# When layer 1's table of finished rows is read, and when it is stored: eight bunches instead of six

## The chip, the cores and the metric

The kernel runs on one core of one Trainium2 chip. The core has five instruction streams that run beside each other and meet only at semaphores: PE (TensorE, matrix products, with its weight loads shown apart as PEld), DVE (VectorE), ACT (ScalarE), POOL (GpSimd, which here does nothing but issue gathers) and SP (SyncE, which here does nothing but issue plain DMAs). The metric is the device time of one execution in microseconds, the median of several runs. A profile is one further execution, recorded by the hardware; its times are microseconds from the first instruction unless marked ns.

## What is computed

A graph with 12,500 nodes of 128 features and 200,000 edges, sorted by the node they end in (`dst`), goes through two relational graph layers, a residual sum and a layer norm. An edge's type is the largest of ten of its 42 attributes.

```python
seg  = dst * NUM_REL + edge_type
sums = segment_sum(x[src], seg);  cnt = segment_sum(1, seg)
mean = (sums / maximum(cnt, 1)).reshape(N, NUM_REL, -1)
layer(x) = einsum('nrd,rdo->no', mean, w_rel) + x @ root + bias
h   = relu(layer_1(x))
out = layernorm(x + layer_2(h))
```

All of it is float32. The feature of an edge's source is fetched by its index (`x[src]`), so a gather from DRAM stands ahead of every sum.

## The kernel before

**Tiles and bunches.** The edges are cut into 1,563 tiles of 128, in the order of `dst`; four tiles (`QB`) make a bunch. For a tile, POOL gathers 128 rows, one for each edge's source (L751). DVE makes a matrix of ones and zeros from the edges' types and nodes, ACT weighs it with one over the count, PE multiplies the gathered rows with it (L983), and DVE adds the product into a ring of sums, `cc` (L797). Gathered rows stand in seven buffers (`GB`) of a bunch each, so POOL can be at most seven bunches ahead of the products.

**Blocks.** The nodes are finished in 52 blocks, most of 256 nodes, that is, about eight bunches of edges each. When the last edges of block k are surely summed, `finish(k)` runs, in the bunch that the code calls `finished_in(k)`: PE multiplies the ring's sums with the ten weight matrices (L739, L742), ACT adds the bias and cuts at zero (`shifted`, L672), PE turns the result back into rows (`rows_out`, L864), and ACT copies the rows to SBUF (`rows_kept`, L871), from where SP stores them in `hD`. Further steps follow by due times that are counted in bunches: the products of layer 2's own part (`second`, three bunches on), their store in `T2` (`second_kept`, four bunches on, L889; the trace calls it T), the clearing of the ring, the next block's features (`fetch`, one bunch on).

**The joint tables.** Layer 2 needs, for the same edges, rows of h in place of rows of x. Part of that is done along with layer 1: from tile `T0` on, POOL gathers from a table `XH` whose rows hold x and, beside it, h as far as it is finished and zeros elsewhere. One gather then feeds two products. An edge whose source is not yet finished contributes nothing to the second product; it is listed and done in layer 2 (the "second" tiles there). So that the list can be made, the kernel fixes for each block from 3 (`K0`) to 43 (`K1`) the tile from which the table is read with this block in it, `first_seen[k]`: `finished_in(k) + READY` bunches, rounded up to a row of eleven tiles (`RT`). The stretch between two such tiles is an epoch. Tiles ahead of `T0` are gathered from x alone, and are done again as a whole in layer 2 (the "plain" tiles there).

**Two copies.** There are two tables, and epochs alternate between them (`table_of`), since the table being read must not change. So each block is stored twice: into the table of its own epoch by `rows_kept` (here called the first copy), and into the other one later, by `todo_late`, two bunches after `first_seen[k]` (the second copy of block k, which the epoch of block k+1 needs). The framework lets a gather wait for all stores in its table that stand ahead of it in the program, and a store for all earlier gathers from its table. Tables are first filled with x and zeros by ACT's queue (`table_rows`, up to bunch 38).

**What sets the order.** The order of instructions on each engine is that of the code: bunch by bunch, and within a bunch POOL's gathers, PE's products, jobs (preparing the edges' types and counts for chunks of 32 bunches), DVE's sums of two bunches before, `finish`, then `todo` and `todo_late`. SP, too, works its queue strictly in this order: whatever stands ahead of a store and waits holds the store up.

**Layer 2** runs over the plain tiles, while DVE compacts the list of left-over edges, and then over the second tiles, with gathers from `hD`.

Of the kernel before, what the change touches and what calls it, by code (L numbers as in the profile page):

```python
# [30 lines left out]
QB = 4  # L31
# [19 lines left out]
SPLIT = 63  # L51
LEAD = 40
LAST = 40
READY = 6
LOW = 1 << 13
TOPN = (1 << 14) - 1
OFF = 80
# [7 lines left out]
def rgcn_resnorm_kernel(ctx: ExitStack, tc: tile.TileContext, x, src, dst, attr, w_rel1, root1, b1,  # L65
# [23 lines left out]
    NBLK = len(starts)  # L89
# [19 lines left out]
    def finished_in(k):  # L109

        return -(-done_after(k) // QB) - 1 + BEHIND

    K0, K1 = KSEEN
    NR = (NT - QB * (finished_in(K0) + READY)) // RT
    T0 = NT - RT * NR
# [4 lines left out]
    for k in range(K0, K1 + 1):  # L120
        r = max(0, -(-(QB * (finished_in(k) + READY) - T0) // RT))
        assert r < NR and (not epochs or epochs[-1][1] < r)
        epochs.append((k, r))
    rows_of = [(k, r, (epochs + [(0, NR)])[i + 1][1]) for i, (k, r) in enumerate(epochs)]
    first_seen = {k: T0 + RT * r for k, r in epochs}
# [62 lines left out]
    def bounds(t):  # L188

        return max(0, t * STEP - OFF, floor_of(t)), min(N - 1, t * STEP + OFF)  # L190
# [43 lines left out]
    def chunk_rows(c):  # L234
        return min(CT, NT - c * CT)
# [96 lines left out]
    first = float(chunk_rows(NCH - 1) * P) - 0.5  # L332
# [288 lines left out]
    def block(k):  # L621
        n0, n = ranges[-1][k]
        return n0, n, [(t, min(P, n - t * P)) for t in range(-(-n // P))]

    def rows_dma(sb, dr, k, store):
        n0, n, _ = block(k)
        full = n // P
        pairs = []
        if full:
            pairs.append((sb[:, :full], dr[n0:n0 + full * P, :].rearrange("(t p) c -> p t c", p=P)))  # L630
        if n % P:
            pairs.append((sb[:n % P, full], dr[n0 + full * P:n0 + n, :]))
        for a, b in pairs:
            nc.sync.dma_start(b, a) if store else nc.sync.dma_start(a, b)
# [3 lines left out]
    def rows_in(k):  # L638

        last = "e" if k == len(ranges[-1]) - 1 else ""  # L640
        xb = fin.tile([P, len(block(k)[2]) if last else 3, C], F32, name="xb" + last)
        rows_dma(xb, x, k, False)
        return xb

    def features_in(k, l, xb):

        n0, n, subs = block(k)
        last = "e" if k == len(ranges[-1]) - 1 else ""
        fT = fin.tile([P, (len(subs) if last else 3) * P], F32, name="fT" + last)
        if l:  # L650
            nc.sync.dma_start(fT[:, :n], hT[:, n0:n0 + n])
            return fT
        pt = ps_f.tile([P, YB], F32, name="pf")
        for t, h in subs:
            nc.tensor.transpose(pt[:, t * P:t * P + h], xb[:h, t, :], ident[:h, :h])
        nc.scalar.activation(fT[:, :n], pt[:, :n], AF.Copy)
        return fT
# [9 lines left out]
    def shifted(po, k, l):  # L667

        n = block(k)[1]
        tail = {NBLK - 1: "e", NBLK - 2: "d"}.get(k, "")  # L670
        a = fin.tile([P, P if tail else 3 * P], F32, name="a" + tail)
        nc.scalar.activation(a[:, :n], po[:, :n], AF.Identity if l else AF.Relu, bias=bsb[l])  # L672
        return a
# [15 lines left out]
    def spans(k):  # L689
        n = block(k)[1]  # L690
        return [(p, slice(a, b)) for p, a, b in ((P, 0, n // P), (n % P, n // P, -(-n // P))) if p and b > a]
# [32 lines left out]
    def folded(ls, k, w):  # L724

        if block(k)[0] % RN or not k:
            return
        s, e = cc[:, ls, :, :w], cc[:, ls, :, RN:RN + w]
        nc.vector.tensor_tensor(s, s, e, op=ALU.add)
        nc.vector.memset(e, 0.0)  # L730

    def projected(k, l, last, po=None, more=True, ring=None):

        n0, n, _ = block(k)
        o = n0 % RN
        if po is None:
            po = ps_f.tile([P, YB], F32, name="pf")
        for r in range(NREL if more else 0):
            nc.tensor.matmul(po[:, :n], wsb[l][:, r, :], cc[:, l if ring is None else ring, r, o:o + n],  # L739
                             start=(r == 0), stop=False)  # L740
        w, f = last
        nc.tensor.matmul(po[:, :n], w, f[:, :n], start=not more, stop=True)  # L742
        return po

    def stored(hb, b, k):

        rows_dma(hb, XH[b][:, C:], k, True)
# [89 lines left out]
    def layer_1():  # L837

        todo = Later()
# [4 lines left out]
        def finish(k, t):  # L844

            if k < NBLK - 2:
                todo.run(END)
            if k not in fTs:
                xbs[k] = rows_in(k)
                fTs[k] = features_in(k, 0, xbs[k])  # L850
            u = QB if t < NT else 0
            folded(ALL, k, WN)
            po = [projected(k, 0, (rsb[0], fTs[k]))]
            both = starts[k + 1] > bounds(T0)[0] if k + 1 < NBLK else True
            reused = starts[k] + RN < N
            assert not reused or t + 7 * u <= (starts[k] + RN - OFF - WN) // STEP

            def rows_out(_):
                a = po.pop()
                a = fin_a.setdefault(k, shifted(a, k, 0))  # L860
                pr = ps_f.tile([P, 4, C], F32, name="pf")
                n0, n, subs = block(k)
                for i, h in subs:
                    nc.tensor.transpose(pr[:h, i, :], a[:, i * P:i * P + h], ident)  # L864
                po.append(pr)

            def rows_kept(now):
                pr = po.pop()
                hb = fin.tile([P, 2, C], F32, name=f"hb{k % 2}")
                for p, s in spans(k):  # L870
                    nc.scalar.activation(hb[:p, s], pr[:p, s], AF.Copy)  # L871
                rows_dma(hb, hD, k, True)
                if k <= K1:
                    first = 0 if k <= K0 else (k - K0) % 2
                    stored(hb, first, k)
                    if k < K1:
                        assert k <= K0 or now + QB >= first_seen[k - 1]
                        when = t + 8 * QB if k < K0 else first_seen[k] + 2 * QB
                        todo_late.append((when, lambda t: stored(hb, 1 - first, k)))

            def second(_):
                po.append(projected(k, 1, (rsb[1], fin_a.pop(k)), more=both))

            def second_kept(_):
                n0, n, _ = block(k)
                p2 = po.pop()
                t2 = fin.tile([P, 3 * P], F32, name="v")
                nc.scalar.activation(t2[:, :n], p2[:, :n], AF.Identity, bias=bsb[1])
                nc.sync.dma_start(T2[:, n0:n0 + n], t2[:, :n])  # L889

            todo.at(t + u, rows_out)
            todo.at(t + (1 if k == NBLK - 2 else 2) * u, rows_kept)
            if reused:
                todo.at(t + 2 * u, lambda t: cleared(0, k, 0))
                todo.at(t + 3 * u, lambda t: cleared(0, k, 1))
            if k < NBLK - 1:
                todo.at(t + (9 if k >= NBLK - 3 else 3) * u, second)
                todo.at(t + (9 if k >= NBLK - 3 else 4) * u, second_kept)
            else:
                todo.run(t)  # L900
                todo.run(END)
                todo.at(t, second)
                todo.at(t, second_kept)
            if both:
                w = 10 if k >= NBLK - 3 else 5
                todo.at(t + w * u, lambda t: cleared(1, k, 0))
                todo.at(t + (w + 1) * u, lambda t: cleared(1, k, 1))
            if k + 1 < NBLK - 1:
                def fetch(t):
                    xbs[k + 1] = rows_in(k + 1)  # L910

                def turn(t):
                    n0, n, subs = block(k + 1)
                    pt = ps_f.tile([P, YB], F32, name="pf")
                    for i, h in subs:
                        nc.tensor.transpose(pt[:, i * P:i * P + h], xbs[k + 1][:h, i, :], ident[:h, :h])
                    po.append(pt)

                def turned_kept(t):
                    n0, n, subs = block(k + 1)  # L920
                    pt = po.pop()
                    fTs[k + 1] = fin.tile([P, 3 * P], F32, name="fT")
                    nc.scalar.activation(fTs[k + 1][:, :n], pt[:, :n], AF.Copy)  # L923
                todo.at(t + u, fetch)
                w = 2 if k == NBLK - 3 else 4
                todo.at(t + w * u, turn)
                todo.at(t + (w + 1) * u, turned_kept)

        fin_a = {}
        todo_late = []  # L930
# [17 lines left out]
        for p in range(-AHEAD, NPT + BEHIND):  # L948
# [9 lines left out]
            t = p * QB  # L958
# [750 lines left out]
```

## Time and profile before

| what | value |
|---|---|
| median of 3 runs | 3995.48 us (3989.87 to 4023.41) |
| the profiled execution: its own time | 4014.34 us |
| its span, first to last instruction | 4012.5 us |
| busy: PE, PEld, DVE, ACT, POOL | 2486.8, 2056.9, 2033.2, 1303.6, 2294.7 us |
| gathers from x (layer 1, to T0), first to last start | 166, 4.0 to 254.3 us |
| gathers from XH (layer 1, from T0 on) | 1397, 292.8 to 2556.9 us |
| gathers from hD, plain tiles of layer 2 | 166, 2583.0 to 2819.7 us |
| gathers from hD, second tiles of layer 2 | 695, 2844.3 to 3927.2 us |
| granted TensorE clock, mean | 0.759 |

No engine is busy for more than 62% of the span, so the time is made of waits as much as of work. In the timeline of the profile each row has the start, the duration, the engine, the line, the operation with what it writes and reads (out<-in), how many instructions were merged, and in brackets how long the engine had been idle before it and what ended that. SPq and ACTq mark instructions that issue a DMA; their duration is that of the issue, not of the transfer. "issue" and "remote" stand for waits whose end the profile does not tell. A gather's row on POOL is the making of its descriptors, and the next gather cannot start before it ends. A wait for several things is put down to the one that came last by the profile. The rows of the windows view have, for each engine, the busy time in a stretch and the number of instructions, then the granted clock, the share of time that the DMA engines worked, and GB/s.

### The profile page before, as it was taken

What the parts mean: (1) busy time and instruction counts of PE and PEld (TensorE: products, weight loads), DVE (VectorE), ACT (ScalarE), POOL (GpSimd) and SP (SyncE); (2) the same over time, 40 slices, a digit from 0 to 9 for tenths busy, and PEclk for the clock granted to TensorE, in tenths of its full rate; (3) what the DMA queues carried; (4) which work ended last, traced back from release to release, by engine and by line L of the source; (5) the groups of instructions that cost most, each with busy time, mean ns of one, the idle gap of its engine ahead of it and who ended that gap; (6) DMA issues with size and microseconds to landing.
All of it is one profiled execution on the core that took longest, in us unless ns stands there. A gap on an engine that the chain in (4) does not pass through costs nothing.

```text
span 4012.5 us, 42414 instructions
## 1 busy us (share of the span) xinstructions
PE 2486.8 (62%) x11883; PEld 2056.9 (51%) x11883; DVE 2033.2 (51%) x5464; ACT 1303.6 (32%) x3179; POOL 2294.7 (57%) x2436
## 2 busy tenths in 40 slices
PE   1555676666665666666676767624546766766666
PEld 0444565555555565555565656614444444545455
DVE  4453454555444546453444344339465555655565
ACT  2341233222332233233332323313324344444443
POOL 6645555565555565655565666466455656665661
PEclk7666777877777777777777877856768887877888
DMA  4562433343333333333333333311112122222121
GB/s 133 176 201 87 125 99 118 96 127 98 121 92 115 104 112 105 112 109 110 109 114 102 98 102 95 89 45 53 42 45 58 54 58 62 59 61 60 56 62 33
DMA packets 265374, 370.96 MB, mean 92 GB/s; under 512 B 51280, under 2 KB 197365, under 8 KB 265134
## 3 DMA queue, kind: packets, MB, share of 16 engines
q0 software_dynamic: 99920, 250.57, 21.4%
q1 hardware_dynamic: 111587, 91.97, 7.4%
q10 hardware_dynamic: 53627, 25.62, 2.2%
q8 instruction: 102, 1.67, 0.2%
q14 instruction: 138, 1.13, 0.1%
HBM read 322.86 MB, written 57.89 MB: 95 GB/s over the span
## 4 chain that ended last, share of the span: by engine, by line
PE 39%; issue 24%; another core or an unknown queue 14%; DVE 14%; ACT 2%; POOL 2%; DVEq 1%; DMA 1%; SPq 0%; ACTq 0%; POOLq 0%
PE zp L983 18%; PE pf L739 13%; DVE cc L797 5%; PE zp L1502 2%; POOL g L751 2%; DVE oh L775 2%; PE zq L1502 1%; PE pf L742 1%; ACT oh L757 1%; DVEq L782 1%; DVE oh L765 1%; DVE cc L1162 1%; PE pf L559 1%; PE pf L557 1%
## 5 line engine op out<-in xcount | busy, mean ns | idle before, releaser
L751 POOL DMA_INDIRECT g<-XH,idxE x1397 | 1321.3, 946 | 981.4 <-issue 444.6
L983 PE MATMUL zp<-oh,g 128*128 128x120 f32 x5920 | 1027.6, 327 | 727.0 <-issue 636.2
L797 DVE TENSOR_TENSOR cc<-cc,zp 128x240 f32 (+11 forms) x2193 | 841.3, 384 | 1150.6 <-remote 662.7
L983 PEld LDWEIGHTS zp<-oh,g 128*128 128x128 f32 x5920 | 943.4, 239 | 813.7 <-issue 731.8
L751 POOL DMA_INDIRECT g<-hD,idxB x695 | 657.1, 945 | 450.5 <-issue 180.6
L739 PE MATMUL pf<-cc,w 128*128 128x256 f32 (+3 forms) x3020 | 767.1, 412 | 174.9 <-issue 82.9
L739 PEld LDWEIGHTS pf<-cc,w 128*128 128x128 f32 x3020 | 616.8, 216 | 305.8 <-issue 113.5
L757 ACT ACTIVATE oh<-oh,wE 128x120 f32<-128x120 f32 x1729 | 531.2, 382 | 352.8 <-DVE oh L765 255.9
L757 ACT ACTIVATE oh<-oh,wB 128x150 f32<-128x150 f32 (+23 forms) x771 | 338.7, 482 | 442.1 <-DVE oh L775 236.4
L1502 PE MATMUL zp<-oh,g 128*128 128x120 f32 (+20 forms) x1260 | 346.8, 418 | 210.2 <-issue 79.8
L1502 PEld LDWEIGHTS zp<-oh,g 128*128 128x128 f32 x1260 | 238.4, 239 | 288.1 <-issue 212.4
L722 ACT ACTIVATE cc<-zero 128x1280 f32<-128x1280 f32 (+3 forms) x274 | 336.6, 1231 | 74.8 <-DVE cc L797 58.2
L775 DVE TENSOR_TENSOR oh<-wide,keyB 128x480 f32<-128x480 f32 (+17 forms) x400 | 230.3, 576 | 177.7 <-remote 100.3
L672 ACT ACTIVATE a<-pf,b 128x256 f32<-128x256 f32 (+1 forms) x50 | 23.2, 465 | 734.5 <-remote 313.8
L765 DVE TENSOR_TENSOR oh<-bank,keyE 128x480 f32<-128x480 f32 x391 | 253.5, 649 | 0.0
L1502 PE MATMUL zq<-oh,g 128*128 128x160 f32 (+21 forms) x614 | 183.3, 433 | 97.4 <-issue 54.9
L751 POOL DMA_INDIRECT g<-hD,idxE x166 | 157.9, 951 | 104.8 <-issue 44.5
L751 POOL DMA_INDIRECT g<-in_x_dram,idxE x166 | 156.8, 945 | 96.2 <-issue 46.9
L1502 PEld LDWEIGHTS zq<-oh,g 128*128 128x128 f32 x614 | 119.7, 229 | 147.3 <-issue 124.1
L797 DVE TENSOR_TENSOR cc<-cc,zq 128x160 f32 (+21 forms) x307 | 120.0, 391 | 61.2 <-issue 14.3
L923 ACT ACTIVATE fT<-pf 128x256 f32<-128x256 f32 (+1 forms) x50 | 18.5, 370 | 401.8 <-remote 344.6
L548 DVE TENSOR_TENSOR eqb<-bank,kh 128x1344 bf16<-128x1344 f32 (+2 forms) x65 | 100.7, 1551 | 25.4 <-remote 19.0
(241 smaller groups left out, 1288.7 us busy)
## 6 DMA issues: line engine op xcount, KB each, us to landing
m<-in_edge_attr_dram SPq DMA_DIRECT2D x48, 672.0 KB
g<-XH,idxE POOLq DMA_INDIRECT x1397
XH<-in_x_dram ACTq DMA_DIRECT2D x24, 512.0 KB
XH<-zero ACTq DMA_DIRECT2D x24, 512.0 KB
XH<-hb SPq DMA_DIRECT2D x87, 128.0 KB
g<-hD,idxB POOLq DMA_INDIRECT x695
xb<-in_x_dram SPq DMA_DIRECT2D x72, 128.0 KB
hD<-hb SPq DMA_DIRECT2D x46, 128.0 KB
```

The costliest lines, as they stand in the source:

```text
L548: nc.vector.tensor_tensor(eq[:p], kpP[:p, None, :R].to_broadcast([p, DB, R]), fore, op=ALU.is_equal)
L557: nc.tensor.matmul(pc[:p], identb[:p, :p], eq[:p, k:k + 4, L:], start=(d + k == 1), stop=False)
L559: nc.tensor.matmul(pc[:p], identb[:p, :p], back, start=False, stop=(d + k + 3 == L))
L722: nc.scalar.activation(cc[:, l, h * H:(h + 1) * H, o:o + n], zero[:, None, :n].to_broadcast([P, H, n]), AF.Copy)
L739: nc.tensor.matmul(po[:, :n], wsb[l][:, r, :], cc[:, l if ring is None else ring, r, o:o + n], start=(r == 0), stop=False)
L751: nc.gpsimd.indirect_dma_start(out=g[:, j * C:(j + n) * C], out_offset=None, in_=table, in_offset=bass.IndirectOffsetOnAxis(ap=idx, axis=0))
L757: nc.scalar.activation(s, s, AF.Copy, scale=w)
L765: nc.vector.tensor_tensor(o.rearrange("p (t m) -> p t m", m=m), cols[:, None, :m].to_broadcast([P, n, m]), keys[:, :, None].to_broadcast([ ...
L775: nc.vector.tensor_tensor(to, a, b, op=ALU.is_equal)
L797: nc.vector.tensor_tensor(s, s, z, op=ALU.add)
L983: nc.tensor.matmul(zp[:, a + l * KW:a + (l + 1) * KW], g[:, (slot[j] + l) * C:(slot[j] + l + 1) * C], oh[:, j * KW:(j + 1) * KW], start=Tr ...
L1502: nc.tensor.matmul(zp[:, j * m:(j + 1) * m], gt[:, b * C:(b + 1) * C], oh[:, j * m:(j + 1) * m], start=True, stop=True)
```

## The change

`READY` goes from 6 to 8: every `first_seen` is computed from eight bunches after the finishing in place of six. `rows_kept` is due one bunch after `finish` for every block, so it stands directly behind `rows_out`; before, it stood a bunch later except for one block. The first copy is stored there only if the table it goes into is no longer read from the next bunch on (`free`); otherwise it waits in `todo_late` until then. The assertion that made this condition a fixed one is gone. The second copy keeps its rule, two bunches after `first_seen[k]`, and moves along with that.

```diff
-READY = 6
+READY = 8
...
                 if k <= K1:
                     first = 0 if k <= K0 else (k - K0) % 2
-                    stored(hb, first, k)
+                    free = first_seen[k - 1] - QB if k > K0 else 0
+                    if now >= free:
+                        stored(hb, first, k)
+                    else:
+                        todo_late.append((free, lambda t: stored(hb, first, k)))
                     if k < K1:
-                        assert k <= K0 or now + QB >= first_seen[k - 1]
                         when = t + 8 * QB if k < K0 else first_seen[k] + 2 * QB
                         todo_late.append((when, lambda t: stored(hb, 1 - first, k)))
...
             todo.at(t + u, rows_out)
-            todo.at(t + (1 if k == NBLK - 2 else 2) * u, rows_kept)
+            todo.at(t + u, rows_kept)
```

## The prediction

> **What bounds the kernel now.** The page's groups of instructions first (busy time, mean ns, then the idle time before them), and the waits of POOL (engine, line, awaited; sum, times, longest in us):
>
> ```profile
> L751 POOL DMA_INDIRECT g<-XH,idxE x1397 | 1321.3, 946 | 981.4 <-issue 444.6
> ```
> ```profile
> POOL g L751 <- issue: 716.6, 2143, 9.7
> POOL g L751 <- remote: 284.0, 96, 10.9
> POOL g L751 <- DMA XH<-hb: 183.5, 27, 16.1
> POOL g L751 <- PE zp L983: 125.1, 38, 12.9
> ```
>
> The 1397 gathers from the joint table are 1321.3 us of work and 981.4 us of idleness. Part of the idleness is the steady step between two gathers. Another part is a wait for a block's rows: the third row says 183.5 us in 27 waits, and some of the waits put down to a product or to "issue" fall at the same places. To see the places, read POOL's timeline at the gathers that open an epoch; I show the first, a few between, and the last.
>
> ```profile
> 292.83 0.94 POOL L751 DMA_INDIRECT g<-XH,idxE  x1 [37.64 <-DMA XH<-zero]
> ...
> 348.61 0.94 POOL L751 DMA_INDIRECT g<-XH,idxE  x1 [11.10 <-DMA XH<-hb]
> ...
> 510.28 0.94 POOL L751 DMA_INDIRECT g<-XH,idxE  x1 [5.93 <-DMA XH<-hb]
> ...
> 883.75 0.94 POOL L751 DMA_INDIRECT g<-XH,idxE  x1 [3.77 <-DMA XH<-hb]
> ...
> 934.89 0.94 POOL L751 DMA_INDIRECT g<-XH,idxE  x1 [3.25 <-DMA XH<-hb]
> ...
> 974.62 0.94 POOL L751 DMA_INDIRECT g<-XH,idxE  x1 [9.75 <-PE zp L983]
> ...
> 1138.15 0.94 POOL L751 DMA_INDIRECT g<-XH,idxE  x1 [9.70 <-issue]
> ...
> 1193.07 0.94 POOL L751 DMA_INDIRECT g<-XH,idxE  x1 [9.81 <-PE zp L983]
> ...
> 2128.89 0.94 POOL L751 DMA_INDIRECT g<-XH,idxE  x1 [16.13 <-DMA XH<-hb]
> ...
> 2339.07 0.94 POOL L751 DMA_INDIRECT g<-XH,idxE  x1 [5.36 <-DMA XH<-hb]
> ...
> 2390.27 0.94 POOL L751 DMA_INDIRECT g<-XH,idxE  x1 [3.68 <-DMA XH<-hb]
> ```
>
> All 40 openings from 348.61 to 2390.27 have such a pause, 3.25 to 16.13 us, 7.2 us in the mean. One epoch shows what is waited for (block 18):
>
> ```profile
> 1077.56 0.47 ACT L672 ACTIVATE a<-pf,b 128x256 f32<-128x256 f32 x1 [12.07 <-PE zp L983]
> ...
> 1079.46 0.38 ACT L871 ACTIVATE hb<-pf 128x256 f32<-128x256 f32 x1 [0.29 <-PE pf L864]
> ...
> 1080.28 0.46 SPq L634 DMA_DIRECT2D XH<-hb  x1
> ...
> 1082.99 0.94 POOL L751 DMA_INDIRECT g<-XH,idxE  x1 [7.77 <-DMA XH<-hb]
> ...
> 1088.76 0.33 SPq L889 DMA_DIRECT2D T<-v  x1
> ```
>
> `rows_kept` at 1079.46, its store at 1080.28, and 2.25 us after the end of that issue (1082.99 − 1080.74) the gather goes on. So at each epoch POOL stands because the newest copy has not landed. But POOL's pause is not PE's. Two stretches after this very pause (the windows view: bounds, length, then PE, PEld, DVE, ACT, POOL):
>
> ```profile
> 1083.00:1092.50 9.50, 9.36 (x63) 8.57 (x62) 6.32 (x16) 3.67 (x11) 7.37 (x8) 1.00 0.70 229
> 1092.50:1105.20 12.70, 1.84 (x8) 1.21 (x7) 2.24 (x6) 0.82 (x1) 9.64 (x11) 0.68 0.35 108
> ```
>
> While POOL issues its first eight gathers, PE does 63 products in 9.5 us; in the next 12.7 us, with POOL still issuing, 8. PE and POOL take turns, and a pause of POOL's is partly paid back. What a pause costs must therefore be read from whole epochs of 33 gathers: 883.75 to 934.89 is 51.14 us, with a pause of 3.25 at its end; 1138.15 to 1193.07 is 54.92 us, with 9.81. That is 3.78 us for 6.56 us of pause, **0.576 us per us**, and 51.14 − 0.576 × 3.25 = 49.3 us for an epoch without any. 2339.07 to 2390.27 tests it: 49.3 + 0.576 × 3.68 = 51.4, measured 51.20.
>
> **The change part by part.**
>
> *How far the reading moves.* By the code's arithmetic an epoch is 33 tiles, a few 22. What decides a pause is the distance in bunches from where the later of its two copies stands in the program to the first gather that reads it. Before, both come at `finished_in` +0 to +3 and the reading at +6.0 to +8.5; the distance is 3.0 at the three openings that follow a 22-tile epoch, 4.25 to 5.25 at 16, 5.5 to 6.25 at 21. After, the first copy comes at +1 (+2 in nine, where `free` holds it back) and the reading at +8.0 to +10.5. The first copy is then 6.0 to 9.25 bunches ahead and no longer decides. The second copy does, since it moves along with `first_seen`: 5.5 to 6.25 bunches at 36 openings, 3.0 at four that follow 22 tiles. So this is not two bunches more for everybody, it is the 16 middle ones brought to where 21 others are already.
>
> *What that is worth.* The 21 openings at 5.5 to 6.25 (first 510.28, last 2390.27) pause 5.5 us in the mean; the 16 at 4.25 to 5.25 8.6 (among them 348.61, 1138.15, 1193.07); the three at 3.0, 9.75 to 16.13. After, I split the 36. In 22 of them the second copy falls at +4 or +5, in SP's queue right behind block k's T2 store (1088.76 for block 18, 8.5 us after the first copy), which waits for products as the first copy did before: I give them the same 5.5. In the other 14 nothing late stands ahead of the copy, and I give them 3.3, the longer of the pauses that POOL makes with no copy in play, seen in the last stretch of the joint gathers:
>
> ```profile
> 2412.01 0.94 POOL L751 DMA_INDIRECT g<-XH,idxE  x1 [3.29 <-remote]
> ...
> 2465.06 0.94 POOL L751 DMA_INDIRECT g<-XH,idxE  x1 [2.08 <-PE zp L983]
> ```
>
> Mean (22 × 5.5 + 14 × 3.3) / 36 = 4.6. A long epoch is then 49.3 + 0.576 × 4.6 = 51.95 us. A short one was 934.89 to 974.62 = 39.73 with 9.75 of pause; I take 40 for each of the four.
>
> *Fewer joint tiles.* `T0` goes from 166 to 177. The pause of 37.64 us at 292.83 is for the zero fill from ACT's queue, which does not move, so the joint gathers start at the same instant, with 11 of them done from x during that pause.
>
> **Sum of the stage.** Before: 2390.27 − 292.83 = 2097.44 us. After: 36 × 51.95 + 4 × 40 = 2030 us. **−67 us.** Bounds: with pauses as now (7.2 in all) the 11 tiles fewer alone are left, 36 × (49.3 + 0.576 × 7.2) + 160 = 2084, −13; with 3.0 everywhere, 36 × 51.03 + 4 × (39.73 − 0.576 × 6.75) = 1981, −117; at the pace of the last stretch (2412.01 to 2465.06, 36 gathers in 53.05 us, 1.474 each) the 1276 gathers take 1881 us, −216. I take −67 because its terms are from epochs of the same kind. The 110 joint tiles behind 2390.27 stay.
>
> *`rows_kept` a bunch sooner.* On ACT, `hb` no longer follows the next bunch's weighting. In the row at 1079.46 it had waited 0.29 us for the transposes already, so there is next to nothing to gain there; a loss is ACT standing for the transposes while weights queue behind it: from 1077.56 + 0.47 to 1079.46, 1.4 us, while PE is at the block's own products anyway. I take 0, bounds −1 to +3 us per block at 0.576. On SP, `hD` and the first copy now stand ahead of `fetch` of the next block's features; those are wanted a block later, so nothing is late.
>
> *Layer 2.* 11 tiles more are plain and 4 second tiles fewer.
>
> ```profile
> L751 POOL DMA_INDIRECT g<-hD,idxB x695 | 657.1, 945 | 450.5 <-issue 180.6
> ```
> ```profile
> 2844.30 1.01 POOL L751 DMA_INDIRECT g<-hD,idxB  x1 [23.66 <-DVE vB L1260]
> ```
>
> 11 gathers of 1.25 us (0.945 + 0.30) are 13.75 us, and lie under the 23.66 us in which POOL waits for DVE's list; without that cover they would cost 13.75. Four second tiles are 4 × (657.1 + 450.5) / 695 = −6.4. I take 0, bounds −6 to +8.
>
> A rule of the Trainium skill speaks against this. Its page "DMA: Bandwidth & Descriptors", section "Queues, rings and completion order", says that each DMA engine takes turns between the queues that have work, packet by packet. Before, the deciding copy landed while POOL stood still (2.25 us above); after, more copies land while gathers run (DMA share 0.70 in the first window above). If that doubled the landing in the 26 epochs behind a T2 store, it would be 2.25 × 26 × 0.576 = +34 us, an estimate, and the forecast 3962; no trace of before shows it, and my sum is without it.
>
> The profile's own run took 4014.34 us; less 67 is 3947. The median of the runs lies 18.86 us lower, so the forecast is 3995.48 − 67 = **3928 us**.
>
> **The rivals.**
>
> *A. POOL runs free.* If a pause's whole length comes off, and POOL settles between my sum and the last stretch's pace, it is half of −67 and −216, about −141: 3854 us. For it: that stretch has the same blocks in it. Against it: the stop-and-go of the two windows does not depend on the copies.
>
> *B. The waits change their name.* Products take their rows from buffers that hold up to seven bunches; the pause at 974.62 already ends on a product and not on a copy. If POOL's pauses are only the other side of PE's turns, they come back as waits for buffers, and the 11 tiles are all that is left: −13, 3982 us. Against it: the long epochs with short pauses are really shorter (51.14 and 51.20 against 54.92). For it: those are three epochs, and which blocks' jobs fall into them differs.
>
> *C. Slower: the second copy behind T2.* Before, the second copy stood within two bunches of the first and ahead of any T2 store of its block. Now 26 times it stands behind a store that waits for ACT's v, at 5.5 to 6.25 (22 epochs) or 3.0 bunches (4). If v is late, the pause grows past what it was. The point from which this decides is a mean pause of 7.2 plus the 13 us of fewer tiles over 40 × 0.576, that is 7.8 for no change, and 9.5 for 40 us slower. At the longest pause seen, 16.13, in those 26 and 3.3 in the others the mean is 11.6 and the stage 4.4 × 40 × 0.576 − 13 = +89: 4084 us; with 13 in the 26, 9.6: +42, 4038 us.
>
> *D. It isn't stored sooner*, since `hb` was bound by the transposes already. My sum has that at nothing, so this alone changes no number.
>
> **How the numbers follow.** Forecast 0.44, own range 3878 to 3965 (pauses of 3.0 everywhere; pauses of 6, 36 × 52.76 + 160 = 2059, −38, with layer 2's +8). A 0.15, B 0.28, C 0.13. 1% is 40 us, about the spread of the three runs (3989.87 to 4023.41) and so about what a measurement can tell from no change. The forecast's weak end reaches into "same", A's weak end is "faster": faster 0.57, same 0.30, slower 0.13. The range leaves out half of A below and most of C above: 3850 to 4015.
>
> **What the profile after would show.** Right: the joint gathers start again near 292.8 and the last epoch opens about 67 us sooner, near 2323; the waits of POOL for XH<-hb fall well below 183.5 us; openings pause 3 to 6 us, the four short ones more; 33 gathers take about 52 us. B: the same pauses put down to products, and epochs of still 53 to 54 us. C: T<-v rows on SP directly ahead of an XH<-hb row, with the gather 2 to 3 us behind, and pauses over 9 us. A: epochs of about 50 us. Wrong in another place: a wait at 2844 longer than 23.66 us, or a first joint gather that is not near 292.8.

## The result, and the profile after

The changed kernel takes **3977.19 us** (median of 12 runs, 3969.64 to 3988.25) against 4002.53 us for the kernel before in the same series (12 runs, 3989.87 to 4023.41): a ratio of **0.9933, 95% interval 0.9918 to 0.9948**. A later series gave 0.9936 (0.9912 to 0.9960). The forecast was 3928, a gain of 67 us; measured were 25 (4002.53 − 3977.19), and 32 in the later series. The direction was right, the size less than half. The profiled execution took 3976.07 us, 38 less than the one before; single executions of one kernel lie up to 19 and 34 us apart in this series, so the medians are the better measure of the whole, and the traces of its parts.

The changed kernel's page, its groups of instructions, and the waits of POOL (sum, times, longest):

```profile
L751 POOL DMA_INDIRECT g<-XH,idxE x1386 | 1311.9, 947 | 928.5 <-issue 405.1
```
```profile
POOL g L751 <- PE zp L986: 125.5, 37, 20.6
POOL g L751 <- DMA XH<-hb: 116.0, 24, 9.1
```

The idle time before joint gathers fell from 981.4 to 928.5 us, the waits put down to a block's rows from 183.5 to 116.0. The longest wait for a product rose from 12.9 to 20.6. Where these stand is seen in POOL's timeline: the first joint gather, the opening that begins a 22-tile epoch and the one that ends it, the ends of two more such epochs, and the last opening.

```profile
311.45 0.94 POOL L751 DMA_INDIRECT g<-XH,idxE  x1 [33.30 <-DMA XH<-zero]
...
775.89 0.95 POOL L751 DMA_INDIRECT g<-XH,idxE  x1 [2.98 <-DMA XH<-hb]
...
822.64 0.94 POOL L751 DMA_INDIRECT g<-XH,idxE  x1 [16.92 <-PE zp L986]
...
1378.59 0.94 POOL L751 DMA_INDIRECT g<-XH,idxE  x1 [13.09 <-PE pf L919]
...
2299.61 0.95 POOL L751 DMA_INDIRECT g<-XH,idxE  x1 [20.61 <-PE zp L986]
...
2351.23 0.94 POOL L751 DMA_INDIRECT g<-XH,idxE  x1 [5.82 <-DMA XH<-hb]
```

Three things are to be read here. The joint gathers start at 311.45, not at 292.83. From there to the last opening are 2039.8 us (forecast 2030, before 2097.4). And the 22-tile epochs are long: 775.89 to 822.64 is 46.75 us, with a pause of 16.92. The 36 epochs of 33 tiles pause 4.68 us in the mean and take 51.55 us; 4.6 and 51.95 were forecast. One opening, of block 20, shows what they wait for:

```profile
1179.23 0.47 ACT L891 ACTIVATE v<-pf,b 128x256 f32<-128x256 f32 x1 [4.46 <-PE pf L742]
...
1179.73 0.33 SPq L892 DMA_DIRECT2D T<-v  x1
1180.12 0.43 SPq L634 DMA_DIRECT2D XH<-hb  x1
...
1182.76 0.95 POOL L751 DMA_INDIRECT g<-XH,idxE  x1 [5.46 <-DMA XH<-hb]
```

ACT's v, its store in T2, right behind it the second copy of block 19, and 2.21 us after that issue's end the gather. Before, the chain at this place was hb, first copy, gather.

### The profile page after: what moved, and what is told of

It is laid out like the page before. It is cut to its first block, busy times and chain, and to the rows that moved or that the text cites. A ratio compares the mean times of both kernels' runs of the same rounds, so it can differ in the third digit from the quotient of the medians.

```text
span 3974.2 us, 42420 instructions
## 1 busy us (share of the span) xinstructions
PE 2451.5 (62%) x11862; PEld 2017.4 (51%) x11862; DVE 2030.5 (51%) x5475; ACT 1305.9 (33%) x3189; POOL 2302.3 (58%) x2443
## 4 chain that ended last, share of the span: by engine, by line
PE 38%; issue 22%; another core or an unknown queue 16%; DVE 15%; ACT 3%; POOL 2%; DMA 1%; DVEq 1%; ACTq 0%; SPq 0%; POOLq 0%
PE zp L986 15%; PE pf L739 14%; DVE cc L797 6%; PE zp L1505 3%; PE zq L1505 2%; ACT oh L757 2%; POOL g L751 2%; DVE oh L775 2%; PE pf L742 1%; DVE oh L765 1%; DVEq L782 1%; PE pf L1197 1%; DVE cc L1165 1%; PE pf L557 1%
## 5 line engine op out<-in xcount | busy, mean ns | idle before, releaser
L751 POOL DMA_INDIRECT g<-XH,idxE x1386 | 1311.9, 947 | 928.5 <-issue 405.1
L797 DVE TENSOR_TENSOR cc<-cc,zp 128x240 f32 (+12 forms) x2190 | 836.2, 382 | 1114.7 <-remote 594.2
L986 PE MATMUL zp<-oh,g 128*128 128x120 f32 x5898 | 958.0, 319 | 524.6 <-issue 409.5
L986 PEld LDWEIGHTS zp<-oh,g 128*128 128x128 f32 x5898 | 893.1, 231 | 597.2 <-issue 461.6
L739 PE MATMUL pf<-cc,w 128*128 128x256 f32 (+5 forms) x3000 | 789.0, 415 | 279.2 <-issue 190.5
L1505 PE MATMUL zp<-oh,g 128*128 128x120 f32 (+22 forms) x1254 | 345.6, 420 | 210.7 <-DVE cc L797 83.0
L1505 PEld LDWEIGHTS zp<-oh,g 128*128 128x128 f32 x1254 | 242.6, 243 | 286.4 <-issue 233.0
L722 ACT ACTIVATE cc<-zero 128x1280 f32<-128x1280 f32 (+1 forms) x274 | 336.2, 1230 | 79.6 <-DVE cc L797 69.8
L775 DVE TENSOR_TENSOR oh<-wide,keyB 128x480 f32<-128x480 f32 (+19 forms) x402 | 228.8, 569 | 227.5 <-remote 147.8
L1505 PE MATMUL zq<-oh,g 128*128 128x140 f32 (+20 forms) x642 | 191.9, 433 | 98.2 <-issue 41.4
L797 DVE TENSOR_TENSOR cc<-cc,zq 128x150 f32 (+20 forms) x321 | 123.9, 386 | 56.3 <-issue 15.1
L891 ACT ACTIVATE v<-pf,b 128x256 f32<-128x256 f32 (+2 forms) x52 | 24.0, 461 | 241.9 <-PE pf L742 107.5
```

What stands on the lines that cost most here:

```text
L722: nc.scalar.activation(cc[:, l, h * H:(h + 1) * H, o:o + n], zero[:, None, :n].to_broadcast([P, H, n]), AF.Copy)
L751: nc.gpsimd.indirect_dma_start(out=g[:, j * C:(j + n) * C], out_offset=None, in_=table, in_offset=bass.IndirectOffsetOnAxis(ap=idx, axis=0))
L775: nc.vector.tensor_tensor(to, a, b, op=ALU.is_equal)
L797: nc.vector.tensor_tensor(s, s, z, op=ALU.add)
L986: nc.tensor.matmul(zp[:, a + l * KW:a + (l + 1) * KW], g[:, (slot[j] + l) * C:(slot[j] + l + 1) * C], oh[:, j * KW:(j + 1) * KW], start=Tr ...
L1505: nc.tensor.matmul(zp[:, j * m:(j + 1) * m], gt[:, b * C:(b + 1) * C], oh[:, j * m:(j + 1) * m], start=True, stop=True)
```

## The experiments

The runs fell on several chips, and these are of two kinds. On three the kernel before takes 3968 to 4013 us, like in the result; on the other two, 3076 to 3081. Several edits were run on both. The table is of the first kind, each ratio against the kernel before on the same chip; the times of the chips differ by about 1%, so rows are best compared within one chip.

| kernel | chip | ratio, 95% interval | first joint gather, us | pause of long epochs, us |
|---|---|---|---|---|
| before, second trace | 11 | 1.0016 (0.9996 to 1.0036) | 295.3 | 6.5 |
| changed, second trace | 11 | 0.9936 (0.9912 to 0.9960) | 311.7 | 4.4 |
| T0 alone moved | 11 | 1.0030 (1.0010 to 1.0051) | 306.6 | 6.8 |
| READY 8 alone | 0 | 0.9857 (0.9834 to 0.9880) | 300.7 | 4.6 |
| rows_kept sooner alone | 0 | 1.0117 (1.0095 to 1.0138) | 303.5 | 7.6 |
| the copy hb sooner alone | 9 | 1.0005 (0.9992 to 1.0018) | 299.3 | 6.4 |
| changed, second copy at once | 11 | 0.9702 (0.9673 to 0.9731) | 312.4 | 1.6 |
| changed, T2 store from ACT | 0 | 0.9750 (0.9731 to 0.9769) | 310.0 | 2.5 |
| both copies sooner, READY 6 | 0 | 0.9991 (0.9974 to 1.0008) | 303.5 | 6.1 |

**Scatter or the program?** Both kernels unchanged, for second traces.

> The kernel before, unchanged, for a second trace. In its first trace the joint gathers start at 292.83 us, in the changed kernel's at 311.41. Theory 1: that is the change's doing (11 tiles more from x, so POOL goes on issuing and PE gets to the bunch of the zero fill later); then this trace has 293 within 3 us again. Theory 2: the early stage scatters from one execution to the next; then it lies anywhere from 290 to 312. Openings of epochs: pauses of 7.2 us in the mean again, within 0.5, if these are set by the program; time equal to before within 0.3%.

> The changed kernel, unchanged, for a second trace. Theory 1 (see the second trace of before): the first joint gather again at 311 within 3 us. Theory 2: anywhere from 290 to 312. Both: the four short epochs again 44 to 48 us and the 36 long ones 51.6 us in the mean; time 0.993 of before.

The start was 295.3 and 311.7: it is the program's. The pauses of before were 7.05 us in the mean again. Over the two pairs of traces, after less before is +17.5 us up to the first joint gather, −61.1 from there to the last opening, −0.7 to the last joint gather, +7.1 behind it: together −37. Medians put the whole at −25 and −32.

**T0 alone.** In the kernel before:

```diff
-    NR = (NT - QB * (finished_in(K0) + READY)) // RT
+    NR = (NT - QB * (finished_in(K0) + 8)) // RT
```

> The kernel before with only T0 moved from 166 to 177 (11 tiles fewer from the joint table, 11 more plain in layer 2, one block fewer with products of layer 2's own part in layer 1); all epochs else, and both copies, as before. Theory 1 (the later start is the change's doing): first joint gather at 311 within 3 us, and the 13 us that 11 tiles are worth are lost again: 1.000 to 1.002 of before. Theory 2 (scatter): first joint gather anywhere from 290 to 312, in the mean as before, and 10 to 20 us less: 0.995 to 0.998 of before.

Nearer to theory 1: the start is later, at 306.6, though not as late as 311 within 3, and the time is a bit worse than expected, +12 us. The stage from the first joint gather to the last opening is 2082.6 us, 13 less than in the two traces of before, as the prediction reckoned for 11 tiles. But it starts 12.5 us later, and layer 2, from the last joint gather to the last of all, is 1382.9 us against 1370.3 and 1361.6. Moving T0 is a cost.

**READY alone, and rows_kept alone.** The two halves of the change; each diff is against the changed kernel.

```diff
-            todo.at(t + u, rows_kept)
+            todo.at(t + (1 if k == NBLK - 2 else 2) * u, rows_kept)
```

> READY 8 alone again. On a chip where before takes about 3080 us (chip 2 of the last runs) 1.0045 again, since no opening pauses there. On one where it takes about 4010 us: theory 1 (the second copy, behind the T2 store, sets the pauses of the changed kernel) long epochs 51.5 us, 0.992 to 0.995; theory 2 (storing a bunch sooner carries the gain) 0.997 to 1.003.

```diff
-READY = 8
+READY = 6
```

> rows_kept a bunch sooner alone, again. At 3080 us: 1.000. At 4010 us: theory 1 (distance in the program decides) 16 x 3.1 x 0.7 = 35 us less, 0.990 to 0.993; theory 2 (hb is bound by the transposes, so a bunch in the program is little in time) 0.996 to 1.000.

READY alone came out at 0.9857, below both expectations: 55 us (3968.46 − 3913.12), near the 67 forecast for the whole. rows_kept a bunch sooner is at 1.0117, on the far side of both: it costs 43 us by itself (4011.13 − 3968.46), and by the difference of 0.9933 and 0.9857 some 30 us (0.0076 × 4000, an estimate: the whole change was not run on the chip of these two) within the change. So most of the gain that was missed went, by this estimate, into the edit that the forecast had at nothing.

**The copy or the stores?** ACT's copy hb was moved and the stores were left:

```diff
                     nc.scalar.activation(hb[:p, s], pr[:p, s], AF.Copy)
-                rows_dma(hb, hD, k, True)
+                po.insert(0, hb)
+
+            def rows_stored(now):
+                hb = po.pop(0)
+                rows_dma(hb, hD, k, True)
...
-            todo.at(t + (1 if k == NBLK - 2 else 2) * u, rows_kept)
+            todo.at(t + u, rows_kept)
+            todo.at(t + (1 if k == NBLK - 2 else 2) * u, rows_stored)
```

> The copy hb alone a bunch sooner, for the third time. Where before takes about 4000 us: theory 1 (ACT standing for the transposes, four weightings behind it) 1.008 to 1.015 of before, first joint gather later than 300 us; theory 2 (the stores) 0.997 to 1.003 and the first joint gather at 293 to 296. Where it takes 3080: 1.000.

1.0005: ACT standing for the transposes costs nothing that can be measured, although the four weightings now stand behind it. The first joint gather, at 299.3, lies between what the two theories said. This ran on another chip than rows_kept sooner, but the two ratios lie over a per cent apart: it is the stores. What they do is seen in SP's timeline. Before, up to one block's store:

```profile
215.54 0.37 SPq L634 DMA_DIRECT2D xb<-in_x_dram  x1
215.97 0.48 SPq L242 DMA_DIRECT2D d_i<-in_dst_dram  x1
216.50 1.30 SPq L461 DMA_DIRECT2D m<-in_edge_attr_dram  x2
218.99 0.33 SPq L242 DMA_DIRECT2D s_i<-in_src_dram  x1
253.01 0.38 SPq L634 DMA_DIRECT2D hD<-hb  x1
```

The same block with rows_kept sooner:

```profile
253.78 0.37 SPq L634 DMA_DIRECT2D hD<-hb  x1
254.20 0.46 SPq L634 DMA_DIRECT2D XH<-hb  x1
254.76 0.92 SPq L634 DMA_DIRECT2D xb<-in_x_dram  x1
255.73 1.68 SPq L242 DMA_DIRECT2D d_i<-in_dst_dram  x1
257.47 1.02 SPq L461 DMA_DIRECT2D m<-in_edge_attr_dram  x2
258.53 0.46 SPq L242 DMA_DIRECT2D s_i<-in_src_dram  x1
```

The same loads for the next chunk's preparation (its edges' nodes, attributes and sources) went out at 216 to 219 us; now they go out in a heap at 255.7 to 258.5. The store is issued when hb is there, 253.01 and 253.78, no sooner. But in SP's queue it now stands a bunch further ahead, so what the jobs of the next bunch load stands behind it and waits with it for hb, 40 us. DVE then waits for them. Its waits for DMAs, first in the kernel before, then with the copy alone sooner, then with rows_kept sooner:

```profile
DVE bank L449 <- DMA m<-in_edge_attr_dram: 5.0, 2, 2.7
DVE s_f L286 <- DMA s_i<-in_src_dram: 1.7, 2, 1.0
```
```profile
DVE bank L449 <- DMA m<-in_edge_attr_dram: 4.9, 2, 2.7
DVE s_f L286 <- DMA s_i<-in_src_dram: 1.7, 2, 1.0
```
```profile
DVE s_f L286 <- DMA s_i<-in_src_dram: 20.0, 4, 10.3
DVE bank L545 <- DMA kh<-KD: 11.4, 4, 5.7
DVE bank L449 <- DMA m<-in_edge_attr_dram: 8.7, 3, 4.2
```

6.7, 6.6 and 40.1 us (one wait of about 16 us in layer 2, which some traces have and some not, is left out). The changed kernel has 41.1 (22.1, 10.7 and 8.3), READY alone 14.7. The 33 us more are of the size of the cost, but that the cost goes this way is not shown. No run moved those loads by themselves, and two runs leave it in doubt: both copies sooner with READY 6, on the same chip as rows_kept sooner, has 39.8 us of these waits (20.4, 10.8 and 8.6) and takes 46.6 us less (4011.13 − 3964.55); and on the other kind of chip rows_kept sooner has 60.0 us of them (24.4, 24.3 and 11.3), the copy alone 14.3, and both take as long as the kernel before.

The stores hold back something else too: the second copy. Before, it mostly stood ahead of the next block's stores or directly beside them. Now it often stands behind them, and behind the loads that wait with them. The opening of block 42 with rows_kept sooner, the queue and the gather (the loads of nodes and attributes from 2346.89 to 2348.64 left out):

```profile
2345.25 0.36 SPq L634 DMA_DIRECT2D hD<-hb  x1
2345.92 0.36 SPq L634 DMA_DIRECT2D XH<-hb  x1
2346.39 0.40 SPq L634 DMA_DIRECT2D xb<-in_x_dram  x1
...
2348.94 0.39 SPq L634 DMA_DIRECT2D XH<-hb  x1
...
2351.89 0.94 POOL L751 DMA_INDIRECT g<-XH,idxE  x1 [11.37 <-DMA XH<-hb]
```

The same opening in the kernel before:

```profile
2335.26 0.39 SPq L634 DMA_DIRECT2D hD<-hb  x1
2335.95 0.89 SPq L634 DMA_DIRECT2D XH<-hb  x2
...
2339.07 0.94 POOL L751 DMA_INDIRECT g<-XH,idxE  x1 [5.36 <-DMA XH<-hb]
```

From the store in hD to the gather it is 6.64 us in place of 3.81. At 38 of the 40 openings of that trace the last store in XH stands directly behind a load in SP's queue; in the kernel before at 2. POOL's waits that are put down to a block's rows (XH<-hb) are 265.2 us there; 183.5 and 168.3 in the two traces of before; 148.7 with the second copy moved out of the way on the same chip. The long epochs pause 7.6 us there, 6.1 with that copy moved, and the stage from the first joint gather to the last opening is 2100.2 and 2050.4 us. So two things are seen to be held up, DVE's loads and the second copy; how the 43 us divide between them stays open.

**What is left of the pauses.** The second copy was put at first_seen[k] itself, and in another kernel the T2 store was given to ACT's queue instead.

```diff
-                        when = t + 8 * QB if k < K0 else first_seen[k] + 2 * QB
+                        when = t + 8 * QB if k < K0 else first_seen[k]
```

> The changed kernel with the second copy at first_seen[k] instead of two bunches after it. It then stands ahead of block k+1's T2 store in SP's queue everywhere (+2 or +3 bunches, before +4 or +5 in 26 epochs). Theory 1 (the copy behind the T2 store sets what is left of the pauses): long epochs' pauses 4.7 to about 3.3 us, short ones' 16 to about 6; with 0.576 us per us that is 22 x 2.0 x 0.576 = 25 us and 4 x 10 x 0.576 = 23 us: 45 to 50 us less than the changed kernel, about 0.981 of before. Theory 2 (what is left are waits for buffers, and taking a copy away only renames them): the pauses at the openings shrink, but the time is that of the changed kernel within 10 us, 0.991 to 0.995 of before.

```diff
-                nc.sync.dma_start(T2[:, n0:n0 + n], t2[:, :n])
+                nc.scalar.dma_start(T2[:, n0:n0 + n], t2[:, :n])
```

> The changed kernel with the T2 store issued by ACT, again. At 3080 us: 1.004. At 4010 us: theory 1 (the wait is for the T2 store ahead of the copy in SP's queue) pauses of long epochs near 1.6 us and 0.970 to 0.974; theory 2 (the place in the program decides) pauses of 4.5 us and 0.992 to 0.995.

0.9702 and 0.9750: both are faster than both kernels, and the second moves no copy at all. So the wait was for the T2 store in SP's queue. (The second is a little off what theory 1 gave: 0.9750 for 0.970 to 0.974, pauses of 2.5 us for 1.6.) The opening of block 20 in each, first with the second copy at once, then with the T2 store from ACT:

```profile
1144.16 0.95 POOL L751 DMA_INDIRECT g<-XH,idxE  x1 [0.30 <-issue]
```
```profile
1139.37 0.95 POOL L751 DMA_INDIRECT g<-XH,idxE  x1 [0.30 <-issue]
```

No pause is left where 5.46 us were. The gain of the first, 89 to 93 us on the changed kernel, is twice what was expected. All openings together fell from 234.8 to 88.2 us, while the longer pauses between them (over 0.6 us) grew from 248.8 to 312.4: less than half came back as waits for something else. And a pause costs more than forecast: long epochs of 53.2 us with 6.7 (the two traces of before) and of 49.55 with 1.57 give 3.62 / 5.12 = 0.71 us per us, not 0.576. This compares two kernels; a straight line through the 37 long epochs of the first trace of before gives 0.65.

**Both copies sooner, the reading not later.** READY 6 and T0 166 as before, rows_kept sooner and the second copy at first_seen[k].

> READY 6 and T0 166 as before, but rows_kept a bunch sooner and the second copy at first_seen[k]: both copies sooner, the reading not later. At 3080 us: 1.000, since no tiles are added to layer 2. At 4010 us: the first copy is 5.0 to 7.5 bunches ahead. Theory 1 (by distance) pauses near 5.5 us, 0.985 to 0.993; theory 2 (only reading later helps) 0.996 to 1.000.

0.9991, theory 2 by the time. By the trace neither is clean: the long epochs take 52.1 us with pauses of 6.1, some less than before, but the start is at 303.5, and the cost of the sooner stores is in it. Against before, the two sooner copies without READY give nothing; against rows_kept sooner alone, the second copy at once gives 46.6 us.

**The other kind of chip.** Nine runs fell there. The changed kernel:

> The changed kernel again. Where before takes about 4000 us 0.990 to 0.996, and about 0.008 above READY 8 alone (0.9857), if the cost of rows_kept adds to the gain of READY; 1.004 where it takes 3080.

1.0037 (1.0024 to 1.0051): slower. The other kernels with READY 8 are alike: READY 8 alone 1.0045, READY 8 with the second copy at once (rows_kept as before) 1.0043, the changed kernel with the T2 store from ACT 1.0041. Those with READY 6 are all at 1.000 within 0.001: rows_kept sooner (twice), the copy sooner (twice), and the second copy alone:

> The kernel before with the second copy at first_seen[k] instead of two bunches after it, nothing else. The first copy, two bunches after finish, is then the later one at all openings (4.0 to 6.5 bunches). Theory 1 (either copy can bind, and before it was the first): long epochs 53 us as before, only the three openings after short epochs gain some us each, 0.996 to 1.000 of before. Theory 2 (the second copy's place was the cost all along): 0.975 to 0.985.

> READY 8, second copy at first_seen[k], rows_kept two bunches after finish as before. Theory 1 (gains and costs add: second copy sooner 0.9702 with the sooner rows_kept, which costs 0.008 to 0.012): 0.958 to 0.964. Theory 2 (the two gains are one and the same, so that the rest is bound elsewhere): 0.968 to 0.974. Where before takes 3080 us: 1.004, by 11 tiles more in layer 2.

So these two expectations were answered only by their last sentence, or not at all: whether the second copy alone would gain on a chip of the first kind, and whether READY 8 with the second copy at once would do better yet without the sooner stores, stays open. What differs is seen in two stretches of equal length in the joint stage (bounds, length, PE, PEld, DVE, ACT, POOL, granted clock, DMA share, GB/s), the changed kernel on the first kind of chip, then on the second:

```profile
1000.00:1022.20 22.20, 12.86 (x57) 10.65 (x56) 6.40 (x15) 2.10 (x7) 14.20 (x15) 0.72 0.30 87
```
```profile
1000.00:1022.20 22.20, 20.41 (x142) 18.69 (x142) 18.54 (x56) 13.19 (x32) 16.91 (x18) 1.00 0.49 137
```

The stretches are not the same piece of the program, and over the whole joint stage the difference is smaller: 7223 products in 2097 us in the kernel before, 7311 in 1611 us with rows_kept sooner on the second kind. In the changed kernel's trace there, POOL issues its joint gathers without a break and never pauses at an opening: 0.30 us is the longest gap at one (a single wait names a copy, of 0.3 us), and the largest group of its waits is the steady step:

```profile
POOL g L751 <- issue: 654.8, 2149, 0.3
```

READY 8 is then 7 gathers more (11 plain, 4 second tiles fewer), 7 × 1.25 = 8.8 us of the 13.5 measured; the rest is not explained.

## Why the prediction was wrong

In the terms of its sum, and by the means of the two pairs of traces: the stage gave −61 us where −67 was forecast, the start of the joint gathers +17.5 where nothing was, and layer 2 +7 where nothing was. Two steps failed: that "the joint gathers start at the same instant", and that moving `rows_kept` costs nothing.

*What bounds the kernel now* held where it was measured: pauses at the openings, set by the newest copy, partly paid back. The mean of before repeated (7.2 and 7.05 us). That PE and POOL take turns was seen on the chips of the first kind alone, which one trace couldn't tell.

*How far the reading moves* and *What that is worth* held best. The second copy behind the T2 store became the one that decides; long epochs paused 4.68 and 4.43 us where 4.6 was worked out, and took 51.55 and 51.42 where 51.95 was. That the mean came out is in part luck: by the order in SP's queue, the 22 behind a T2 store paused 4.95 and 4.62 us where 5.5 was given, the 14 others 4.27 and 4.14 where 3.3 was; nothing late was to stand ahead of these, and loads held up by the sooner stores did. The price per us was too low (0.576; 0.65 within one trace, 0.71 between two kernels). The short epochs were mis-sized: 40 us taken, 46.0 and 44.4 measured in the mean of four in the two traces, some 20 us in all. Their pauses stand 3.0 bunches behind a T2 store, not behind a first copy, and were 13 to 21 us, more than most seen before. The long epochs were shorter than forecast by about as much (0.4 and 0.5 us in each of 36), so that the stage of 2030 was met (2039.8 and 2029.0) by two errors that offset each other.

*Fewer joint tiles* failed. The zero fill "does not move" in the program, but ACT comes to it later: its last fill is issued at 288.5 us before and at 300.5 with T0 alone. The 11 gathers more from x fill the pause in which PE caught up before, and the joint gathers start at 306.6 with T0 alone. The 13 us were in the stage, and were lost ahead of it. *Layer 2* was taken at nothing, with +8 as its bound; T0 alone gave +17 there (1382.9 against the mean of 1366.0), the changed kernel +7, which is within the 9 us between the two traces of before.

***rows_kept* a bunch sooner** is the step that cost most by the runs of single edits. The sum had it at 0, for two reasons. The first, on ACT, was right (1.0005 with the copy alone). The second was "on SP, `hD` and the first copy now stand ahead of `fetch` of the next block's features; those are wanted a block later, so nothing is late". It looked at one thing queued behind the store and missed the others: the loads of the jobs of the next bunch, which run ahead of `finish`'s steps in each bunch, and so had gone out before the store that waits for hb; and the second copies, which came to stand behind that store and those loads. DVE's waits for DMAs grew by 33 us, and the edit costs 43 us by itself and an estimated 30 within the change. How much of this goes through the loads and how much through the second copies, no run shows.

The rivals: C was the right mechanism (T2's store ahead of the second copy) with the wrong price; it didn't make the kernel slower, since the first copies had been waited for just as long, but it held back another 73 to 93 us (0.9936 against 0.9750 and 0.9702). B, that waits only change their name, is refuted on this kind of chip by the 0.9702: less than half came back elsewhere. D was true, as stated (in the median hb came 2.2 and 1.8 us after the shifting in the two traces of before, 1.5 with rows_kept sooner); what it left out, a store that is earlier in the queue while hardly earlier in time, comes with the cost.

The rule of the Trainium skill that was weighed, "DMA: Bandwidth & Descriptors", section "Queues, rings and completion order", on engines that take turns between queues: the deciding copies of the changed kernel landed as fast as before (2.21 us from the end of issue to the gather, 2.25 before). POOL still stood while they did, so this trace doesn't test it.

## What to carry to other kernels

When a store that waits is moved ahead in an in-order DMA queue, list everything that it is moved past on that queue, loads for other parts of the kernel and copies that someone waits for first of all: a store a bunch sooner in the program was hardly sooner in time, and what it was moved past went out later. When a reading is moved later, look at which of its several producers becomes the last, and what stands ahead of that one in its queue; here a store of another table did, and taking it out of the way was worth nearly three times the change itself. And a term "hidden in a pause" is worth nothing before it is known what else used the pause to catch up.

## What the hardware showed

The same program takes 3968 to 4013 us on three chips and 3076 to 3081 on two others. What differs in the traces is how PE fares while POOL issues gathers. PE's waits of the kernel before, in its own trace, and of the kernel with the second copy alone sooner, on the other kind of chip:

```profile
PE zp L983 <- issue: 636.2, 482, 24.0
```
```profile
PE zp L983 <- issue: 73.2, 23, 18.4
```

"issue" is a wait for nothing that the profile shows. A stretch like the second of the two windows shown with the prediction, with 11 gathers too, but on the second kind (the second copy alone sooner):

```profile
809.50:822.20 12.70, 12.24 (x61) 10.65 (x60) 3.60 (x10) 1.61 (x5) 9.65 (x11) 0.75 0.43 129
```

There PE does 61 products in 12.7 us while POOL issues 11 gathers, on the first kind 8 in the same time. The granted clock is 0.75 here and 0.68 there, so in these two stretches the clock alone is not the difference. The cause isn't settled by any run. It decides the verdict: the same change is 0.7% faster on one kind and 0.4% slower on the other, and the kernel with the T2 store from ACT, 2.5% faster on the first, is 0.4% slower on the second.
